# A cross-attention layer with layer norm: first transfer of context and key weights split in two, an input block queued ahead of output weights, one batch's masks cast at once, and GpSimd passes tied behind VectorE passes

## The chip, the core and the metric

The kernel runs on one core of a Trainium2 chip. The core has five engines with a queue of instructions each, done in order: TensorE (PE, matrix products; PEld is its loading of weights), VectorE (DVE), ScalarE (ACT), GpSimd (POOL) and SyncE (SP, which here only issues DMAs). ACT and POOL issue some DMAs too. An engine waits for another by semaphores. PE writes to PSUM, which has eight banks of 128 x 512 float32; everything else lives in SBUF, and inputs and outputs in HBM.

The metric is the device time of one execution in microseconds. Verdicts compare medians of several executions; the profile comes from one execution whose own time is given beside it.

## What is computed

```python
def _L0_xattn_ref(q, k, v, wq, wk, wv, wo, gamma, beta, mask):
    B, S, D, H = (2, 1024, 512, 16); HD = D // H
    Bq, Lq, _ = q.shape; Lk = k.shape[1]
    qs = (q @ wq).reshape(Bq, Lq, H, HD).transpose(0, 2, 1, 3)
    ks_ = (k @ wk).reshape(Bq, Lk, H, HD).transpose(0, 2, 1, 3)
    vs = (v @ wv).reshape(Bq, Lk, H, HD).transpose(0, 2, 1, 3)
    scores = jnp.einsum('bhqd,bhkd->bhqk', qs, ks_) / jnp.sqrt(jnp.float32(HD))
    scores = jnp.where(mask[:, None, :, :], -jnp.inf, scores)
    attn_w = jax.nn.softmax(scores, axis=-1)
    attn = jnp.einsum('bhqk,bhkd->bhqd', attn_w, vs)
    attn = attn.transpose(0, 2, 1, 3).reshape(Bq, Lq, H * HD)
    out = attn @ wo + q
    mu = jnp.mean(out, axis=-1, keepdims=True)
    var = jnp.mean((out - mu) ** 2, axis=-1, keepdims=True)
    return (out - mu) / jnp.sqrt(var + EPS) * gamma + beta
```

`q` is x, 4 x 2048 x 512 float32; `k` and `v` are both the context, 4 x 77 x 512; the mask is 4 x 2048 x 77. There are 16 heads of 32.

## The kernel before

**Tiles and stages.** The 8192 rows of x make 64 tiles of 128 rows, 16 to a batch. Two tiles are a block (32 blocks, `b`), four are a group of 512 rows (16 groups, `g`), for which q is computed at one go.

**Split products.** Products with wq, wk, wv and wo are made in three parts for accuracy: each operand is split into a high part (cast to fp32r) and a low part (what the cast lost), and high x high, high x low and low x high are summed in a bank. A split is a cast, mostly by ACT, and a subtraction by DVE or POOL.

**The order.** Nothing is scheduled by a planner at build time. The text `ORDER` lists words in the order in which instructions are issued; each engine does its own in that order. `SLOTS` lists the buffer that each allocation takes, `"mm"` those of the eight PSUM banks. A word is a letter, a number and sometimes a part: `T39.2` is part 2 (a quarter of the heads) of tile 39. The words that matter here, with the engine and the line in the profile:

- `l0 l2` (SP, L707): load the second input block, group 1, into `stage_a`, over the staged context and keys' weights; `g` (SP, L263): load half of a later group. `i` (ACT, L266): its cast. `j` (POOL, L270): its low part. A number k is group k // 2, half k % 2, so `i2 i3 j2 j3` are group 1, `i4 i5 j4 j5` group 2, `j23` half of group 11.
- `R` (SP, L359): load a quarter of wo for the low part, 256 KB; `p` (POOL's DMA, L362): load wo's high part, cast on the way, 1 MB; `G` (DVE, L368): wo's low part. `A` (SP, L347), `C` (POOL's DMA, L350), `F` (DVE, L356): the same for wv. `E` (POOL, L353): a copy that holds POOL's DMAs until wq has landed.
- `L` (SP, L377): load a batch's mask bytes. `M28.4` (DVE, L386): turn those of tiles 28 to 31 into a bf16 bias. `M` has no dependence on POOL.
- `H`, `Q` (PE, L276): a visit, a quarter of a group's q; `I`, `q` (DVE, L292 and L290): its copy out of PSUM. `H0 H2 I0 I2` are the second half of group 0.
- `S` (PE, L403): scores of a tile, into four banks. `T` (DVE, L420): add the mask, take the maxima and copy to SBUF, which frees the bank of that quarter. `e` (ACT, L435): exponentials and their sums. `r` (DVE, L445): reciprocals. `n` (POOL, L450): scale by them. `t` (DVE, L471): transpose in blocks of 32. `P`, `U`: DMAs that regroup the result, mostly SP's.
- `B` (PE, L327): values; `D` (DVE, L336): their copy. `V` (PE, L496): values' product of a block, in two banks. `a` (ACT, L525) and `b` (DVE, L529): its high and low parts. `O` (PE, L552): output product of a tile. `x` (SP): load x for the residual. `+` (DVE, L561): add it. `s` (DVE, L575 and L576): moments. `v` (POOL, L581 to L584): 1 / sqrt of a block's variances. `k` (ACT, L590): scale by them. `f` and `)` (POOL, L593 and L596): gamma and beta. `w` (SP): store.

**The start.** Ahead of `ORDER`, PE runs nine matmuls on a constant. SP queues, in this order, four chunks of `kin` (context and wk side by side, 308 + 512 columns each, into `stage_a`), the first half block of x with wq in between, the mask of batch 0, and the other half block. Chunk by chunk the context and wk are split (L666 to L672) and `keys_part` makes the keys' products; then wq and x are split and `q` of the first 256 rows is made. The tail of that part is:

```python
    for c in range(0, NC_D, 2):
        split(xh[0][:, c : c + 2, BLK:], xl[0][:, c : c + 2, BLK:], f0[c][:, 1])
    for m in range(0, NG, 2):
        nc.scalar.copy(qd[0][:, m, :BLK], pq0[m][:, :BLK])
        nc.vector.tensor_copy(qd[0][:, m + 1, :BLK], pq0[m + 1][:, :BLK])
```

Then the words of `ORDER` follow. Its first ones are:

```
R1 R0 R3 E l0 l2 C2 C0 C1 C3 g5 M4.4 A0 M0.1 M12.4 A1 M1.3 A3 M8.4 A2 H2 p i3 g4 i2 S0 I2 j2 S1 T0.1 e0.1
```

**Around 276 us** the order has `r35 O26 a14.0 b14.0 n34 t34 O27 +27 v12 P16.7s Q43 q43 M44.4 e36.2 k24 a14.1 b14.1 n35 t35 i22 s27 V15 x28 )23 f24 e36.1 S37 T37.3 T37.2 k25 a15.0 b15.0 T37.1`, five regrouping and store words, `M40.4 j23 f25 )25`, and on to `e37.1 +26 s26 v13`, `T37.0`, `j22`, `n36`, `k27 a15.1 b15.1 )24 S38`.

Of the kernel before, what the change touches and what calls it, by code (L numbers as in the profile page):

```python
# [8 lines left out]
F32 = mybir.dt.float32  # L9
# [4 lines left out]
ALU = mybir.AluOpType  # L14
# [35 lines left out]
R1 R0 R3 E l0 l2 C2 C0 C1 C3 g5 M4.4 A0 M0.1 M12.4 A1 M1.3 A3 M8.4 A2 H2 p i3 g4 i2 S0 I2 j2 S1 T0.1 e0.1  # L50
T0.2 H0 T0.0 j3 e0.0 T1.0 T0.3 e0.2 T1.1 Q4 T1.2 e0.3 F0 T1.3 I0 e1.2 r0 n0 S2 q4 e1.0 S3 T2.3 T2.0 Q7 T2.2 L1 R2 F3
Q6 F1 G1 x1 e1.1 F2 i5 j5 g7 t0 e1.3 Y1 r1 n1 T3.1 T3.2 T2.1 q7 B0 T3.3 i4 t1 P0.7s P0.3s P0.10s j4 D0 Z3.s Z0.s G2 G3
G0 g6 P0.11s Q5 q6 q5 e2.0 e2.3 e3.3 e2.2 e2.1 e3.1 i7 j7 B2 r2 T3.0 e3.0 S4 T4.2 T4.0 T4.3 n2 T4.1 e4.2 D2 P0.1s e3.2
r3 n3 e4.3 e4.0 P0.6s P0.5s i6 j6 e4.1 g8 P0.8s Z2.s P0.9s P0.4s B1 D1 P0.2s t2 P0.0s t3 P1.10s P1.11s S6 T6.0 T6.3
T6.2 P1.2s r4 P1.3s P1.1s Q10 T6.1 e6.0 Q8 q8 n4 e6.2 e6.1 e6.3 q10 Q9 q9 Z1.s S5 T5.0 e5.0 P1.6s P1.7s P1.5s P1.0s
P1.4s P1.8s t4 S7 T7.1 e7.1 T7.3 T7.2 e7.2 P1.9s r6 n6 T7.0 e7.0 T5.2 Y0 Z15.s Z10.s Q14 Q11 g9 q11 T5.1 T5.3 e7.3 r7
n7 t6 x7 Z16.s e5.2 Q13 q14 i8 e5.3 S9 T9.1 Z4.s V1 t7 x0 x3 P3.9s P3.11s P3.4s Z14.s a1.0 b1.0 x2 e5.1 r5 n5 j8 q13
a1.1 b1.1 T9.2 T9.0 Z5.s V0 a0.0 b0.0 T9.3 P3.0s P3.5s e9.1 e9.0 a0.1 e9.3 i9 j9 P3.10s P3.7s P3.8s O2 t5 M28.4 S8
T8.1 e8.1 T8.2 e8.2 e9.2 +2 b0.1 s2 O3 +3 P2.5s T8.3 e8.3 T8.0 e8.0 P3.2s r9 s3 v1 P2.3s P3.3s Z11.s k3 P2.0s P3.1s
# [15 lines left out]
P9.4s a7.0 b7.0 e20.3 P8.6s Q24 q24 P9.9s O13 e21.0 i15 j15 a7.1 v5 e21.1 e22.1 )9 +13 s13 Q26 q26 b7.1 e20.1 r20 n20
w8 e21.3 e21.2 T22.3 r21 k10 f10 O12 +12 s12 t20 n21 e22.0 w5 P9.1s P9.6s f4 )4 e22.3 P9.7s w9 Q27 q27 e22.2 P9.10s
P9.3s S23 T23.1 T23.3 T23.2 e23.3 P9.0s v6 g17 P9.5s x15 V8 a8.0 a8.1 i16 e23.1 k11 S24 t21 P10.1s O15 r22 b8.1 n22
b8.0 P10.0s w4 x17 T24.0 T24.2 e24.2 O17 O16 T24.1 e23.2 T23.0 e23.0 T24.3 +15 P10.9s x14 x16 t22 P10.4s k12 r23 e24.3
S25 T25.0 T25.3 T25.2 k13 +17 s17 e25.2 e24.1 P10.3s )10 P10.8s f11 P10.6s P10.2s P10.11s n23 t23 T25.1 V9 a9.1 a9.0
# [10 lines left out]
e31.0 r31 n31 P14.1s P14.4s e32.2 i21 P14.8s w19 k20 f20 j21 )20 k21 f21 e32.1 T32.3 e32.3 w16 x25 P14.5s P14.2s T32.0  # L90
t30 P14.0s P14.10s x24 e32.0 O23 +23 O22 +22 b12.0 s23 Q38 q38 S33 T33.2 T33.3 T33.1 V13 i20 S34 e33.2 P14.9s t31
P15.5s P14.7s P14.11s s22 v11 )21 e33.3 T34.1 T33.0 e33.0 O24 a13.0 b13.0 j20 r32 n32 +24 k22 e33.1 a13.1 T34.2 k23
T34.0 g22 P15.9s P15.6s e34.2 P15.11s P15.7s r33 T34.3 e34.3 e34.0 f22 Q39 q39 b13.1 n33 Q36 q36 t32 O25 +25 S35 T35.2
T35.3 e34.1 g23 P15.10s w20 w21 P15.1s P15.4s P15.0s f23 T35.1 T35.0 e35.1 V14 P15.8s )22 r34 P15.3s P15.2s t33 P16.2s
P16.4s S36 T36.3 s24 T36.2 s25 T36.0 e35.2 e35.0 i23 e35.3 T36.1 r35 O26 a14.0 b14.0 n34 t34 O27 +27 v12 P16.7s Q43
q43 M44.4 e36.2 k24 a14.1 b14.1 n35 t35 i22 s27 V15 x28 )23 f24 e36.1 S37 T37.3 T37.2 k25 a15.0 b15.0 T37.1 P16.6s
P16.1s P16.3s P16.8s w22 P16.0s M40.4 j23 f25 )25 x29 x26 P16.11s e36.0 e36.3 e37.1 +26 s26 v13 e37.3 e37.2 w23
P16.10s x31 T37.0 r36 O29 +29 s29 j22 O28 +28 s28 P16.9s P17.10s w25 n36 x32 P16.5s k27 a15.1 b15.1 )24 S38 T38.3
T38.1 T38.0 k26 e37.0 T38.2 e38.3 e38.2 r37 n37 f26 )26 Q41 q41 Q42 q42 e38.1 t36 P17.11s g25 P17.0s P17.2s Q40 q40
S39 T39.1 P17.4s T39.2 T39.0 T39.3 e38.0 t37 e39.1 x30 r38 f27 v14 n38 i25 g24 )27 P17.6s P17.9s V16 a16.1 e39.0 e39.2  # L100
S40 T40.1 P17.3s i24 P17.5s w24 T40.0 b16.1 T40.2 O30 O31 T40.3 P18.5s P17.1s P17.7s P17.8s a16.0 P18.10s Q44 w26
P18.1s e40.0 e39.3 b16.0 O32 k29 e40.2 P18.8s x34 +30 j24 +31 s31 e40.3 s30 v15 k31 t38 r39 P18.6s n39 q44 w27 S41
T41.0 P18.11s f29 P18.9s e40.1 V17 P18.4s L3 x33 g26 j25 f31 Q45 t39 P18.2s P19.10s e41.0 T41.2 P18.0s P18.3s a17.1
T41.3 P19.7s e41.3 k30 k28 +32 T41.1 P19.4s P18.7s q45 S42 T42.1 )31 a17.0 e42.1 e41.2 e41.1 T42.0 T42.3 r40 s32 O33
# [70 lines left out]
def xattn_layernorm(  # L175
# [92 lines left out]
    def split_xT(g, c):  # L268
        l = once(xl, g, [P, NC_D, GRP], F32R, "xtl")
        nc.gpsimd.tensor_tensor(l[:, c : c + 2], fx.pop((g, c)), xh[g][:, c : c + 2].bitcast(F32), ALU.subtract)  # L270
# [517 lines left out]
```

## Time and profile before

| | |
|---|---|
| median of 3 executions | 513.0 us (512.81, 513.0, 514.88) |
| the profiled execution | 513.14 us |
| its span, first to last instruction | 511.3 us, mean granted clock of PE 0.998 |
| busy: PE, PEld | 499.2 us (98%), 383.9 us (75%) |
| busy: DVE, ACT, POOL | 470.3 us (92%), 464.6 us (91%), 421.1 us (82%) |
| DMA | 110.85 MB, mean 217 GB/s |

The span is shorter than the time of its execution by 1.8 us, which lie before the first and behind the last instruction. In rows of the trace the first number is the start in us from the span's start, the second the length in us; then the engine (SPq is SP's queue of DMAs), the line, the operation, what it writes and reads, the shapes and the count of instructions that the row merges. Brackets give the engine's idle time before it and what ended it. In rows of waits, "PE sc L403 <- DVE q L290" is PE's instruction of line 403 waiting for DVE's of line 290. Ends of matmuls are modelled, so the distance between starts says more than a matmul's length.

### The profile page before, as it was taken

How to read it: one execution, taken by the hardware profiler on the slowest of the kernel's cores; microseconds unless marked ns; L12 is line 12 of the kernel's file. 1: busy time of each engine (PE TensorE's matmuls, PEld its weight loads, DVE VectorE, ACT ScalarE, POOL GpSimd, SP SyncE). 2: the span in 40 equal slices, each digit the busy share in tenths (PEclk: the TensorE clock that was granted, in tenths of full speed). 3: DMA queues.
4: the chain of work that ended last, by engine and by line, in shares of the span. 5: the costliest groups of instructions: out<-in, count | busy, mean ns of one | idle time of the engine just before them, and what ended most of it. 6: DMA issues, size and time to landing. Idle time of an engine off the chain costs nothing. (4 is left out here: it accounts for less than half of the span.)

```text
span 511.3 us, 20308 instructions
## 1 busy us (share of the span) xinstructions
PE 499.2 (98%) x6833; PEld 383.9 (75%) x6833; DVE 470.3 (92%) x2563; ACT 464.6 (91%) x2222; POOL 421.1 (82%) x387
## 2 busy tenths in 40 slices
PE   8998999999999999999999999999999999999994
PEld 6976777777777877777777777778777777777773
DVE  5799889988999989988989998999999999999997
ACT  6698999999999999998999999999999999989720
POOL 2556656876897999998898899898999899898896
PEclk9999999999999999999999999999999999999999
DMA  8954786878686986779877868787879677699655
GB/s 307 390 196 131 173 220 163 230 177 225 192 245 182 267 222 169 229 210 249 245 223 210 228 172 252 178 219 204 247 201 235 189 217 240 192 228 252 162 185 216
DMA packets 58781, 110.85 MB, mean 217 GB/s; under 512 B 9462, under 2 KB 11278, under 8 KB 58678
## 3 DMA queue, kind: packets, MB, share of 16 engines
q1 hardware_dynamic: 55222, 102.75, 72.0%
q0 software_dynamic: 2496, 5.77, 4.0%
q8 instruction: 54, 0.88, 0.8%
q10 hardware_dynamic: 960, 1.05, 0.8%
q14 instruction: 49, 0.40, 0.3%
HBM read 41.79 MB, written 16.78 MB: 115 GB/s over the span
## 5 line engine op out<-in xcount | busy, mean ns | idle before, releaser
L435 ACT ACTIVATE pbuf<-pbuf,nm 128x77 f32<-128x77 f32 x1024 | 352.7, 352 | 8.7 <-DVE nm L420 8.0
L435 ACT ACTIVATION_READ_ACCUMULATOR pbuf<-pbuf,nm 128x1 f32 x1024 | 197.1, 193 | 0.0
L420 DVE CUSTOM_DVE_ANT_0 pbuf<-sc,mb 128x77 f32<-128x77 f32 x1024 | 170.0, 231 | 6.4 <-PE sc L403 4.6
L450 POOL TENSOR_TENSOR pbuf<-pbuf,ri 128x1232 f32<-128x1232 f32 x63 | 142.3, 2261 | 34.8 <-DVE ri L445 29.6
L552 PE MATMUL po<-woh,AH 128*128 128x512 f32 x256 | 104.0, 406 | 0.1
L471 DVE STREAM_TRANSPOSE B<-pbuf 128x1280 f32<-128x1280 f32 x64 | 95.8, 1498 | 8.2 <-POOL pbuf L450 7.2
L276 PE MATMUL pq<-xth,wqh 128*128 128x512 f32 (+1 forms) x256 | 100.6, 393 | 0.9 <-DVE nm L420 0.6
L552 PE MATMUL po<-wol,AH 128*128 128x512 f32 x256 | 100.0, 391 | 0.0
L552 PE MATMUL po<-woh,AL 128*128 128x512 f32 x256 | 99.9, 390 | 0.0
L276 PE MATMUL pq<-xtl,wqh 128*128 128x512 f32 (+1 forms) x256 | 98.2, 383 | 0.0
L276 PE MATMUL pq<-xth,wql 128*128 128x512 f32 (+1 forms) x256 | 98.1, 383 | 0.0
L420 DVE DVE_READ_ACCUMULATOR2_ANT nm<- 128x1 f32 x1024 | 84.4, 82 | 0.0
L270 POOL TENSOR_TENSOR xtl<-xtf,xth 128x1024 fp32r<-128x1024 f32 x28 | 67.4, 2408 | 9.6 <-issue 4.8
L593 POOL TENSOR_TENSOR o<-o,gam 128x512 f32<-128x512 f32 x56 | 72.1, 1292 | 2.9 <-ACT o L590 2.7
L596 POOL TENSOR_TENSOR o<-o,bet 128x512 f32<-128x512 f32 x56 | 72.0, 1289 | 1.4
L403 PEld LDWEIGHTS sc<-kct,q 32*64 32x64 f32 x4096 | 51.8, 130 | 24.4 <-issue 11.5
L403 PE MATMUL sc<-kct,q 32*64 32x77 f32 x4096 | 61.7, 238 | 2.2 <-DVE q L290 1.6
L496 PE MATMUL pa<-PT,vsb 96*32 96x256 f32 x992 | 59.7, 382 | 0.0
L552 PEld LDWEIGHTS po<-woh,AH 128*128 128x128 f32 x256 | 48.0, 188 | 15.3 <-issue 3.8
L276 PEld LDWEIGHTS pq<-xth,wqh 128*128 128x128 f32 x256 | 48.1, 188 | 14.7 <-issue 2.1
L552 PEld LDWEIGHTS po<-woh,AL 128*128 128x128 f32 x256 | 48.1, 188 | 10.5
L276 PEld LDWEIGHTS pq<-xth,wql 128*128 128x128 f32 x256 | 48.1, 188 | 9.6
(99 smaller groups left out, 640.3 us busy)
## 6 DMA issues: line engine op xcount, KB each, us to landing
PT<-B SPq DMA_DIRECT2D x343, 128.0 KB
xtf<-xT SPq DMA_DIRECT2D x28, 512.0 KB
o<-x SPq DMA_DIRECT2D x56, 256.0 KB
out<-o SPq DMA_DIRECT2D x56, 256.0 KB
PT<-B POOLq DMA_DIRECT2D x25, 128.0 KB, 4.8
stage_a<-kin SPq DMA_DIRECT2D x4, 410.0 KB
xtf<-xT SPq DMA_DIRECT2D x4, 256.0 KB
wq_f<-wq SPq DMA_DIRECT2D x4, 256.0 KB
```

Of the source, the lines that this page charges most:

```text
L270: nc.gpsimd.tensor_tensor(l[:, c : c + 2], fx.pop((g, c)), xh[g][:, c : c + 2].bitcast(F32), ALU.subtract)
L276: nc.tensor.matmul(pq, w[:, c, m * P : (m + 1) * P], r[g][:, c, rs], start=(n == 0), stop=(n == 11))
L403: mm = nc.tensor.matmul(sc[j][r0 : r0 + SR, g * NK : (g + 1) * NK], qs[q, g, rs.start + r0 : rs.start + r0 + SR], kct[q, g, t // TPB, keys ...
L420: nc.vector.tensor_tensor_reduce(pb[:, h // 2, (h % 2) * NK : (h % 2 + 1) * NK], scs[t][j][:, g * NK : (g + 1) * NK], mb[:, t % TPB, keys_ ...
L435: nc.scalar.activation(pb[:, h // 2, (h % 2) * NK : (h % 2 + 1) * NK], pb[:, h // 2, (h % 2) * NK : (h % 2 + 1) * NK], AF.Exp, bias=nmax[t ...
L450: nc.gpsimd.tensor_tensor(pv, pv, rv.to_broadcast((P, NP, 2, NK)), ALU.mult)
L471: nc.vector.transpose(bt.rearrange("p c q r -> p q c r"), pbuf[t % NPB].rearrange("p q (c r) -> p q c r", c=5),)
L496: nc.tensor.matmul(pas[b, g // 2][HD * j : HD * (j + 1), (g % 2) * BLK : (g % 2 + 1) * BLK], vsb[:, 2 * b // TPB, h % 2, HD * (h // 2) : H ...
L552: nc.tensor.matmul(pos[t], a[:, c, rs], w[:, c, :], start=(first and c == 0 and n == 0), stop=(c == NC_D - 1 and n == 2),)
L593: nc.gpsimd.tensor_tensor(od[t], od[t], gam, ALU.mult)
L596: nc.gpsimd.tensor_tensor(od[t], od[t], bet, ALU.add)
```

## The change

- The first chunk of `kin` comes in two transfers: the context and the first half of wk's columns, then the other half. Its wk is cast and split by halves, and the keys' products of chunk 0 are made for the first two of four banks (all three parts), then for the other two.
- `E l0 l2` stand ahead of `R1 R0 R3` in the order.
- The masks of batch 0 are made by one instruction over its 16 tiles, ahead of the copies of the first q, in place of five words `M`.
- A new wait: after each word `F`, `G` or `M`, the next word `j`, `n`, `f` or `)` waits for it to end. `split_xT`, `split_wv`, `split_wo`, `mask_bias`, `normalise`, `gain` and `shift` return their instruction for that.
- `SLOTS`: from the scores of tile 1 on, banks 6 and 7 are exchanged; the last of "PT" is changed, and isn't taken by any allocation.

```diff
 ORDER = """
-R1 R0 R3 E l0 l2 C2 C0 C1 C3 g5 M4.4 A0 M0.1 M12.4 A1 M1.3 A3 M8.4 A2 H2 p i3 g4 i2 S0 I2 j2 S1 T0.1 e0.1
+E l0 l2 R1 R0 R3 C2 C0 C1 C3 g5 A0 A1 A3 A2 H2 p i3 g4 i2 S0 I2 j2 S1 T0.1 e0.1
...
     def keys_part(pks, c):
         terms = ((woh, 0), (woh, 1), (wol, 0))
-        steps = [(n, m) for n in range(3) for m in range(NG)] if c == 0 else [(n, m) for m in range(NG) for n in range(3)]
+        steps = [(n, m) for m in range(NG) for n in range(3)]
+        if c == 0:
+            steps = [(n, m + i) for m in (0, 2) for n in range(3) for i in (0, 1)]
...
+    def wait_for(later, earlier, reason):
+        info = mybir.DependencyInfo(mybir.DependencyClass.Sync, mybir.DependencyReason.DATA)
+        tc.add_manual_dep(later.ins, earlier.ins.name, info, reason=reason)
...
-    for c in range(NC_D):
+    half = NB * NK + D // 2
+    nc.sync.dma_start(kin_f[:, 0, :half], kin[:, 0, :half])
+    nc.sync.dma_start(kin_f[:, 0, half:], kin[:, 0, half:])
+    for c in range(1, NC_D):
         nc.sync.dma_start(kin_f[:, c], kin[:, c])
...
         if c == 0:
             nc.vector.tensor_copy(ctx_s[c][0], ctx_f)
-            nc.scalar.copy(woh[:, c], wk_f)
-            nc.vector.tensor_tensor(ctx_s[c][1], ctx_f, ctx_s[c][0].bitcast(F32), ALU.subtract)
-            nc.vector.tensor_tensor(wol[:, c], wk_f, woh[:, c].bitcast(F32), ALU.subtract)
+            for h in range(2):
+                cols = slice(h * D // 2, (h + 1) * D // 2)
+                nc.scalar.copy(woh[:, c, cols], wk_f[:, cols])
+                if h == 0:
+                    nc.vector.tensor_tensor(ctx_s[c][1], ctx_f, ctx_s[c][0].bitcast(F32), ALU.subtract)
+                nc.vector.tensor_tensor(wol[:, c, cols], wk_f[:, cols], woh[:, c, cols].bitcast(F32), ALU.subtract)
...
+    mask_bias(0, TPB)
     for m in range(0, NG, 2):
         nc.scalar.copy(qd[0][:, m, :BLK], pq0[m][:, :BLK])
...
+    shared = None
     for word in ORDER.split():
...
         else:
-            ops[op](int(k or 0), int(part or 0))
+            ins = ops[op](int(k or 0), int(part or 0))
+            if op in "FGM":
+                shared = ins
+            elif shared and op in "jnf)":
+                wait_for(ins, shared, "VectorE's pass over two tiles of SBUF is begun ahead of GpSimd's")
+                shared = None
```

More of the change, by code (lines that the diff above doesn't have):

```diff
@@ L55 @@
[L55 to L59, printed above, removed]
@@ L75 @@
[L75 to L79, printed above, removed]
@@ L90 @@
[L90 to L104, printed above, removed]
@@ new lines @@
+T22.1 T22.2 s10 g16 T22.0 s11 x12 P8.7s P9.11s e20.0 f8 f9 )8 P9.8s P9.2s P8.0s P9.4s a7.0 b7.0 e20.3 P8.6s Q24 q24
+P9.9s O13 e21.0 i15 j15 a7.1 v5 e21.1 e22.1 )9 +13 s13 Q26 q26 b7.1 e20.1 r20 n20 w8 e21.3 e21.2 T22.3 r21 k10 f10 O12
++12 s12 t20 n21 e22.0 w5 P9.1s P9.6s f4 )4 e22.3 P9.7s w9 Q27 q27 e22.2 P9.10s P9.3s S23 T23.1 T23.3 T23.2 e23.3 P9.0s
+v6 g17 P9.5s x15 V8 a8.0 a8.1 i16 e23.1 k11 S24 t21 P10.1s O15 r22 b8.1 n22 b8.0 P10.0s w4 x17 T24.0 T24.2 e24.2 O17
+O16 T24.1 e23.2 T23.0 e23.0 T24.3 +15 P10.9s x14 x16 t22 P10.4s k12 r23 e24.3 S25 T25.0 T25.3 T25.2 k13 +17 s17 e25.2
@@ new lines @@
+P15.1s P15.4s P15.0s f23 T35.1 T35.0 e35.1 V14 P15.8s )22 r34 P15.3s P15.2s t33 P16.2s P16.4s S36 T36.3 s24 T36.2 s25
+T36.0 e35.2 e35.0 i23 e35.3 T36.1 r35 O26 a14.0 b14.0 n34 t34 O27 +27 v12 P16.7s Q43 q43 M44.4 e36.2 k24 a14.1 b14.1
+n35 t35 i22 s27 V15 x28 )23 f24 e36.1 S37 T37.3 T37.2 k25 a15.0 b15.0 T37.1 P16.6s P16.1s P16.3s P16.8s w22 P16.0s
+M40.4 j23 f25 )25 x29 x26 P16.11s e36.0 e36.3 e37.1 +26 s26 v13 e37.3 e37.2 w23 P16.10s x31 T37.0 r36 O29 +29 s29 j22
+O28 +28 s28 P16.9s P17.10s w25 n36 x32 P16.5s k27 a15.1 b15.1 )24 S38 T38.3 T38.1 T38.0 k26 e37.0 T38.2 e38.3 e38.2
@@ new lines @@
+r37 n37 f26 )26 Q41 q41 Q42 q42 e38.1 t36 P17.11s g25 P17.0s P17.2s Q40 q40 S39 T39.1 P17.4s T39.2 T39.0 T39.3 e38.0
+t37 e39.1 x30 r38 f27 v14 n38 i25 g24 )27 P17.6s P17.9s V16 a16.1 e39.0 e39.2 S40 T40.1 P17.3s i24 P17.5s w24 T40.0
+b16.1 T40.2 O30 O31 T40.3 P18.5s P17.1s P17.7s P17.8s a16.0 P18.10s Q44 w26 P18.1s e40.0 e39.3 b16.0 O32 k29 e40.2
+P18.8s x34 +30 j24 +31 s31 e40.3 s30 v15 k31 t38 r39 P18.6s n39 q44 w27 S41 T41.0 P18.11s f29 P18.9s e40.1 V17 P18.4s
+L3 x33 g26 j25 f31 Q45 t39 P18.2s P19.10s e41.0 T41.2 P18.0s P18.3s a17.1 T41.3 P19.7s e41.3 k30 k28 +32 T41.1 P19.4s
@@ L355, in split_wv @@
     def split_wv(c):
-        nc.vector.tensor_tensor(wvl[c], stage_b[:, 0, c], wvh[c].bitcast(F32), ALU.subtract)
+        return nc.vector.tensor_tensor(wvl[c], stage_b[:, 0, c], wvh[c].bitcast(F32), ALU.subtract)
     def load_wo(c):
@@ L367, in split_wo @@
     def split_wo(c):
-        nc.vector.tensor_tensor(wol[:, c], stage_b[:, 1, c], woh[:, c].bitcast(F32), ALU.subtract)
+        return nc.vector.tensor_tensor(wol[:, c], stage_b[:, 1, c], woh[:, c].bitcast(F32), ALU.subtract)
     def idents():
@@ L391, in early_waits @@
         for part in parts[int(after[1:])] if after[0] == "V" else ():
-            info = mybir.DependencyInfo(mybir.DependencyClass.Sync, mybir.DependencyReason.DATA)
-            tc.add_manual_dep(mm.ins, part.ins.name, info, reason="values' product waits ahead of the scores")
+            wait_for(mm, part, "values' product waits ahead of the scores")
     def scores(t):
@@ L592, in gain @@
     def gain(t):
-        nc.gpsimd.tensor_tensor(od[t], od[t], gam, ALU.mult)
+        return nc.gpsimd.tensor_tensor(od[t], od[t], gam, ALU.mult)
     def shift(t):
-        nc.gpsimd.tensor_tensor(od[t], od[t], bet, ALU.add)
+        return nc.gpsimd.tensor_tensor(od[t], od[t], bet, ALU.add)
     def store(t):
```

161 lines of the change are left out of this document (86 added, 75 removed).

## The prediction

> **What bounds the kernel now.** I read the busy times by stage first, then TensorE's own waits, then the order of time on each engine at those waits. The cuts at 62, 276 and 306 us are mine; behind a stretch and its length stand the busy times of PE, PE's weight loads, DVE, ACT and POOL, the clock, the DMA share and GB/s.
>
> ```profile
> 0.00:62.00 62.00, 58.13 (x788) 47.76 (x789) 51.71 (x261) 49.77 (x223) 32.77 (x30) 1.00 0.77 243
> 276.00:306.00 30.00, 29.41 (x416) 22.57 (x415) 29.59 (x163) 29.53 (x136) 27.40 (x25) 1.00 0.77 213
> ```
>
> TensorE (PE) is the bound: it idles 3.9 us of the first 62 and 0.6 of the 30 behind 276. Only what moves a PE wait, or makes one, moves the end. VectorE (DVE) and ScalarE (ACT) are nearly full from 276 to 306, so little there absorbs a delay.
>
> ```profile
> PE sc L403 <- DVE q L290: 1.6, 2, 1.3
> PE pk L300 <- ACT woh L667: 0.5, 1, 0.5
> PE pq L276 <- DVE nm L420: 0.6, 1, 0.6
> ```
>
> The columns are the total in us, the times and the longest. PE's waits are few and short: 1.3 and 0.3 us for copies of q, 0.5 at the first keys' product, 0.6 for the maxima that free a bank; these 2.7 us are 0.5% of the time.
>
> **First chunk in two transfers.** The rows are PE's, DVE's and ACT's, in order of time.
>
> ```profile
> 5.08 0.83 PE L300 MATMUL pk<-ctx_h,woh 128*128 128x308 f32 x4 [0.45 <-ACT woh L667]
> 7.17 0.41 PE L300 MATMUL pk<-ctx_h,wol 128*128 128x308 f32 x1
> 6.42 0.69 DVE L249 TENSOR_TENSOR wol<-stage_a,woh 128x512 fp32r<-128x512 f32 x1
> 5.42 0.45 ACT L248 CAST ctx_h<-stage_a 128x308 fp32r<-128x308 f32 x1 [0.39 <-DMA stage_a<-kin]
> ```
>
> PE can start some 0.45 us sooner, right behind the warm-up. But the low part of chunk 1's weights is ready at 6.42 + 0.69 = 7.11, in a chain that starts with that chunk's landing (ACT waits for it until 5.42), and the matmul that takes it starts right then, at 7.17. The same bytes stand ahead of chunk 1, so PE waits there instead: 0 gained. Bounds: 0.45 gained if chunk 1 also comes earlier, 0.45 lost if the extra issue delays it. I take 0, the row at 7.17.
>
> **Second input block ahead of three output weights.**
>
> ```profile
> 9.86 1.67 SPq L359 DMA_DIRECT2D stage_b<-wo  x3
> 7.43 0.69 DVE L249 TENSOR_TENSOR wol<-stage_a,woh 128x512 fp32r<-128x512 f32 x1
> 18.00:21.00 3.00, 3.00 (x48) 2.87 (x54) 1.69 (x7) 0.84 (x2) 0.00 (x0) 1.00 1.16 397
> 20.16 1.99 ACT L266 CAST xth<-stage_a 128x1024 fp32r<-128x1024 f32 x2 [2.16 <-DMA stage_a<-xT]
> 22.24 4.75 POOL L270 TENSOR_TENSOR xtl<-stage_a,xth 128x1024 fp32r<-128x1024 f32 x2 [5.92 <-ACT xth L266]
> 26.16 1.39 DVE L356 TENSOR_TENSOR wvlAH<-stage_b,wvh 128x512 fp32r<-128x512 f32 x1
> 28.09 0.68 DVE L292 COPY q<-pq 128x512 f32<-128x512 f32 x1
> 28.83 1.67 PE L403 MATMUL sc<-kct,q 32*64 32x77 f32 x128 [0.37 <-DVE q L292]
> ```
>
> Three transfers of 256 KB at 397 GB/s are 2.0 us, just the time that ACT is idle. The casts `i3 i2` move from 20.16 to about 18.15, GpSimd's (POOL) two splits from 22.24 to about 20.2, and end at 24.9 instead of 26.99. `F0` at 26.16 then meets no POOL pass. It took 1.39 where its kind takes 0.68, ending 0.55 behind POOL's end, so 0.7 goes. The copy behind it ends 0.7 sooner, before PE is free: the 0.37 wait goes, and q's next product takes its place. **Gain 0.4** (0 if the block lands no sooner, 0.5 at most). On SP's queue the block passes three transfers, to 9.86. It overwrites `stage_a`, whose chunk 2 DVE has read by 7.43 + 0.69 = 8.1, so SP is not held there. The weights land where the block did, about 20, and `G1` reads them at 32.93.
>
> **Masks of batch 0 at once.**
>
> ```profile
> 17.27 0.42 DVE L694 COPY q<-pq 128x256 f32<-128x256 f32 x1 [0.88 <-PE pq L680]
> 18.33 1.23 DVE L386 TENSOR_SCALAR mb<-m 128x384 bf16<-128x384 uint8 x5
> ```
>
> The 1.23 us move in front of the copy of q, into the 0.88 us of idle time there; the copies end 0.3 later or not at all. PE has a whole visit of q (`H2`, 24 matmuls) to do before its scores use them: 0. If that cover were gone, 0.3.
>
> **The ties early on.** A word `F`, `G` or `M` (a DVE pass) is now waited for by the next POOL word of `j n f )`.
>
> ```profile
> 32.79 2.49 POOL L270 TENSOR_TENSOR xtl<-xtf,xth 128x1024 fp32r<-128x1024 f32 x1 [1.53 <-ACT xth L266]
> 32.93 2.90 DVE L368 TENSOR_TENSOR wol<-stage_b,woh 128x512 fp32r<-128x512 f32 x1
> 43.14 1.88 DVE L368 TENSOR_TENSOR wol<-stage_b,woh 128x512 fp32r<-128x512 f32 x3
> 44.94 1.28 DVE L290 COPY q<-pq 128x512 f32<-128x512 f32 x2
> 44.54 0.39 PE L403 MATMUL sc<-kct,q 32*64 32x77 f32 x16
> 46.27 0.82 PE L403 MATMUL sc<-kct,q 32*64 32x77 f32 x48 [1.34 <-DVE q L290]
> ```
>
> `G1` began 0.14 us behind POOL's `j5` and took 2.90, 2.2 more than its kind. Now `j5` waits for `F2`, which DVE does behind `F1` and `G1`. With the 0.7 from above DVE is 2.9 sooner: it ends `G1` at 35.83 - 2.9 = 32.9 and `F2` at 33.6. `j5` runs from 33.6 to 36.1, 0.8 later than before; `n1`, queued behind it, takes 2.26 (as at 276.47 below) to 38.4; `j4`, another split of 2.4, runs to 40.8. DVE's `t1` waits for `n1`. Its place is a transpose (1.49) and a copy (0.68) ahead of `G2`, that is 43.14 - 2.9 - 2.1 = 38.1, so it waits 0.3. `G2` then comes at 40.5 and meets the last 0.3 of `j4`. Of 2.9 us 2.3 are left: the two copies of q end at 46.22 - 2.3 = 43.9. PE reaches them at 44.1 and no longer waits: a quarter of the scores' 64 matmuls was through ahead of the wait, the other 48 would have started some 0.25 after 44.54, not at 46.27. **Gain 1.5** (bounds 0 and 1.6).
>
> **The ties later.** POOL, DVE, ACT, PE around 276 us; last, all passes over masks.
>
> ```profile
> 276.47 2.26 POOL L450 TENSOR_TENSOR pbuf<-pbuf,ri 128x1232 f32<-128x1232 f32 x1
> 281.31 2.40 POOL L270 TENSOR_TENSOR xtl<-xtf,xth 128x1024 fp32r<-128x1024 f32 x1
> 285.03 1.29 POOL L596 TENSOR_TENSOR o<-o,bet 128x512 f32<-128x512 f32 x1
> 288.17 0.20 POOL L581 TENSOR_TENSOR rn<-mv,small 128x2 f32<-128x2 f32 x1 [1.84 <-DVE mv L576]
> 279.53 0.67 DVE L386 TENSOR_SCALAR mb<-m 128x384 bf16<-128x384 uint8 x1
> 280.72 1.49 DVE L471 STREAM_TRANSPOSE B<-pbuf 128x1280 f32<-128x1280 f32 x1
> 285.39 1.15 DVE L386 TENSOR_SCALAR mb<-m 128x384 bf16<-128x384 uint8 x1
> 289.72 0.82 ACT L590 ACTIVATE o<-o,rn 128x512 f32<-128x512 f32 x1 [0.40 <-POOL rn L584]
> 290.44 0.57 ACT L525 CAST AH<-pa 128x512 fp32r<-128x512 f32 x1
> 291.79 0.66 DVE L529 TENSOR_TENSOR AL<-pa,AH 128x512 fp32r<-128x512 f32 x1
> 299.45 0.08 DVE L420 DVE_READ_ACCUMULATOR2_ANT nm<- 128x1 f32 x1
> 299.88 0.83 PE L403 MATMUL sc<-kct,q 32*64 32x77 f32 x54
> ...
> L386 DVE TENSOR_SCALAR mb<-m x17: 204/354/2109, 18.3 to 446.5; 128x384 bf16<-128x384 uint8 x15, 128x96 bf16<-128x96 uint8 x1, 128x288 bf16<-128x288 uint8 x1
> ```
>
> Here POOL is ahead of the written order. `n35` began at 276.47, but the word before it that ties it, `M44.4`, comes to DVE at 279.53, behind a copy of q that waits for PE. `n35` now starts at 279.53 + 0.35 = 279.9, 3.4 late. Queued behind it on POOL stand `)23 f24 j23 f25 )25 v13`; on DVE `t35` waits for it until 282.2, 1.5 late. That puts the next mask, `M40.4`, at 286.9 to 287.25 (0.7 late in the end, since no POOL pass stretches it now), and PE's 0.6 us wait for a bank grows by 0.7. `j23` is tied to `M40.4`: 287.3 instead of 281.31. With its 2.40, two passes of 1.29 behind it and 1.55 for `v13` (288.17 to ACT's 289.72) that is 293.9. ACT's `k27` waited for just that already, so it is 4.2 late, and with it `a15.1`. `a15.1` ended at 291.0, DVE's `b15.1` began 0.8 later, at 291.79, so it is 3.4 late; DVE has next to no idle time from there to the maxima of tile 39, whose second group ends at 299.53 and frees a bank of `S40`, 0.35 before PE starts it at 299.88. PE comes 3.4 - 0.35 = **3.1 late** in all, and PE has nothing to catch up with. Bounds: 0.7 if ACT and DVE swallow `k27`'s delay, 4.2 if none of it is absorbed.
>
> The other ten masks: the longest, 2.11 us, is one that POOL's `n45`, begun just ahead, blocked; the tie gives DVE 2.11 - 0.35 = 1.75 and delays POOL by less, both where PE has no wait. The rest are past before POOL's next word, or shift POOL by up to 2 us in stretches where it idles afterwards: 0 each, 0.3 either way together. `SLOTS` only renames two banks.
>
> By the Trainium skill (SBUF — State Buffer, § Who interferes with whom) a VectorE instruction with two SBUF inputs and a GpSimd one that reads SBUF exclude each other, and whichever comes second waits for the first one's end. The trace agrees (2.90 against 0.68 us). The rule speaks against a tie: the exclusion alone costs the second at most the first one's length, while the tie also charges POOL for the way of DVE to the pass, 3.4 us at `n35`; without that charge the time would be the first rival's.
>
> **Sum.** The profiled execution took 513.14 us (span 511.3 and 1.8 around it), 0.14 above the median of 513.0. 513.14 + 0 - 0.4 + 0 - 1.5 + 3.1 = 514.3; beside the median, **514.2**.
>
> **Rivals.**
> - *The late ties are hidden.* If POOL's delay at 276 is swallowed, only the early gain is left: 513.0 - 1.9 = 511.1, and 510.4 with the small waits too (0.3 at 60 us, 0.2 later). For it: POOL is idle 1.84 us before `v13` and DVE had 0.7 us of collisions to lose. Against it: ACT already waits for `v13`, and DVE is busy 29.59 of 30 us there.
> - *The output weights come late (slower).* `G1` reads two transfers of them: SP's, now behind the input block, and POOL's, whose rows are these (issue; size and time to landing):
>
> ```profile
> 15.51 0.81 POOL L362 DMA_DIRECT2D woh<-wo  x1
> woh<-wo POOLq DMA_DIRECT2D x1, 1024.0 KB, 15.3
> ```
>
>   It landed at 15.5 + 15.3 = 30.8; `G1` is now to start at 32.2. If the new order of transfers delays it by over 1.4 us, `G1` waits, and by its tie `F2` also `j5`, `n1`, `t1` and the copies of q. 0.2 us more use up PE's margin, and from there each us costs one: at 33.9 the 1.5 is lost, 513.0 - 0.4 + 3.1 = 515.7. For it: 30.8 is near. Against it: the block and the weights swap places well ahead of that, so the bytes in front of this transfer stay the same.
> - *The early parts do nothing*, since the block lands no sooner: the 0.4 and a part of the 1.5 stay away, 514.8 to 515.3. DMA at 397 GB/s with that block at the end of its queue speaks against it.
>
> **Chances.** A measurement of this kernel tells about 0.5% (2.6 us) from no change, so the edges are 510.4 and 515.6. Forecast, 513.2 to 515.3: 0.52, all within. Late ties hidden: 0.27, of which 0.10 below 510.4. Output weights late: 0.13, of which 0.10 above. Early parts idle: 0.08, of which 0.04 above. So faster 0.10, same 0.76, slower 0.14. The range reaches to both first rivals: 510.7 to 516.0; the likeliest case alone is 513.2 to 515.3.
>
> **What would show it.** Right: PE's first keys' matmul near 4.6 but chunk 1's third no sooner; ACT's cast of the second block near 18.2; the passes of L368 and L356 all at 0.68; no PE wait near 46; then POOL idle some 3 us before `n35`, ACT waiting some 3 us for `rn` before a L590, and a PE wait of over 2 us at the scores of tile 40. Wrong: `n35` starting right behind `v12`, or ACT's wait there staying at 0.4.

## The result and the profile after

| | before | after |
|---|---|---|
| median, us | 513.16 (6 runs, 512.81 to 514.88) | 522.28 (6 runs, 519.84 to 523.0) |
| profiled execution, us | 513.14 | 522.27 |
| its span, us | 511.3 | 520.2 |
| its mean granted clock of TensorE | 0.998 | 0.989 |

The ratio is 1.0167, with a 95% interval of 1.0143 to 1.0191. The changed kernel is slower by 9.1 us, where 1.2 were forecast and 516.0 was the upper end of the range. Three single executions of 693 to 1689 us (one of the run with `M52.4` alone, two of the kernel before) are slow ones and stand outside the comparisons below.

The stretches with the cuts of the prediction, in the kernel after:

```profile
0.00:62.00 62.00, 60.57 (x794) 50.40 (x795) 50.59 (x265) 51.59 (x232) 32.57 (x30) 1.00 0.80 249
276.00:306.00 30.00, 26.97 (x401) 20.03 (x400) 25.28 (x141) 25.33 (x119) 23.98 (x22) 1.00 0.65 185
```

In the first 62 us PE is busy 60.57 us instead of 58.13: the early part gains. In the 30 us behind 276 PE idles 3.0 us instead of 0.6, and DVE, ACT and POOL are all less busy than before: each waits for another.

Then the two largest groups of waits that are new in kind, and PE's waits over 1 us behind its warm-up (total, times, longest):

```profile
POOL pbuf L455 <- DVE mb L388: 9.2, 5, 3.5
POOL o L601 <- DVE mb L388: 6.3, 2, 4.5
...
PE sc L408 <- DVE nm L425: 1.8, 3, 1.1
PE po L557 <- ACT pbuf L440: 1.6, 1, 1.6
PE sc L408 <- DVE o L566: 1.2, 1, 1.2
PE po L557 <- DVE nm L425: 1.2, 2, 0.9
PE sc L408 <- DVE q L290: 1.1, 1, 1.1
```

POOL now waits for masks (`mb`), which no POOL word did before: L455 is the normalisation `n`, L601 the word `)`. The longest, 4.5 us, is at a mask to which the prediction gave a cost of 0.

Where the time went is read by following the same matmul through both traces. First of before, then of after, PE's rows:

```profile
17.79 0.28 PE L276 MATMUL pq<-xth,wqh 128*128 128x256 f32 x1
47.02 0.50 PE L327 MATMUL pv<-wvh,ctx_h 128*128 128x512 f32 x1
300.76 0.50 PE L552 MATMUL po<-woh,AH 128*128 128x512 f32 x1
370.24 0.63 PE L496 MATMUL pa<-PT,vsb 96*32 96x256 f32 x7
458.82 0.50 PE L552 MATMUL po<-woh,AH 128*128 128x512 f32 x1
461.74 0.48 PE L403 MATMUL sc<-kct,q 32*64 32x77 f32 x26
```

```profile
18.70 0.28 PE L276 MATMUL pq<-xth,wqh 128*128 128x256 f32 x1
29.28 1.76 PE L408 MATMUL sc<-kct,q 32*64 32x77 f32 x128
45.80 0.51 PE L329 MATMUL pv<-wvh,ctx_h 128*128 128x512 f32 x1
302.73 0.50 PE L557 MATMUL po<-woh,AH 128*128 128x512 f32 x1
373.48 0.42 PE L501 MATMUL pa<-PT,vsb 96*32 96x256 f32 x4
465.74 0.77 PE L557 MATMUL po<-woh,AH 128*128 128x512 f32 x1 [1.57 <-ACT pbuf L440]
471.12 0.39 PE L408 MATMUL sc<-kct,q 32*64 32x77 f32 x16
```

After minus before: +0.9 at the first products of q, +0.45 at the scores that stood at 28.83, -1.2 at the values' products, +2.0 behind 300 us, +3.2 at 370, +6.9 at 459 and +9.4 at 462. So the start loses 0.9, the early part gains 2.1, and from there 3.2 us are lost around 276 to 303, 1.3 more by 370 and 6.1 more by 462. The last step, 2.5 us within twelve matmuls, is no wait at all: see the section on the clock.

### The profile page after: what moved, and what is told of

Same layout as the page of the kernel before. It is cut to its first block, busy times and chain, and to the rows that moved or that the text cites. A ratio compares the mean times of both kernels' runs of the same rounds, so it can differ in the third digit from the quotient of the medians.

```text
span 520.2 us, 20318 instructions
## 1 busy us (share of the span) xinstructions
PE 504.3 (97%) x6833; PEld 387.7 (75%) x6833; DVE 463.7 (89%) x2560; ACT 464.5 (89%) x2223; POOL 420.2 (81%) x387
## 3 DMA queue, kind: packets, MB, share of 16 engines
q10 hardware_dynamic: 960, 1.05, 0.8%
## 5 line engine op out<-in xcount | busy, mean ns | idle before, releaser
L440 ACT ACTIVATION_READ_ACCUMULATOR pbuf<-pbuf,nm 128x1 f32 x1024 | 200.2, 196 | 0.0
L455 POOL TENSOR_TENSOR pbuf<-pbuf,ri 128x1232 f32<-128x1232 f32 x63 | 142.0, 2257 | 38.3 <-DVE ri L450 23.4
L601 POOL TENSOR_TENSOR o<-o,bet 128x512 f32<-128x512 f32 x56 | 71.9, 1289 | 7.7 <-DVE mb L388 6.3
L408 PE MATMUL sc<-kct,q 32*64 32x77 f32 x4096 | 62.9, 238 | 4.3 <-DVE nm L425 1.8
L595 ACT ACTIVATE o<-o,rn 128x512 f32<-128x512 f32 x56 | 44.7, 815 | 13.8 <-POOL rn L589 12.4
```

Source lines behind the costliest of these rows:

```text
L408: mm = nc.tensor.matmul(sc[j][r0 : r0 + SR, g * NK : (g + 1) * NK], qs[q, g, rs.start + r0 : rs.start + r0 + SR], kct[q, g, t // TPB, keys ...
L440: nc.scalar.activation(pb[:, h // 2, (h % 2) * NK : (h % 2 + 1) * NK], pb[:, h // 2, (h % 2) * NK : (h % 2 + 1) * NK], AF.Exp, bias=nmax[t ...
L455: return nc.gpsimd.tensor_tensor(pv, pv, rv.to_broadcast((P, NP, 2, NK)), ALU.mult)
L595: nc.scalar.activation(o, o, AF.Identity, bias=rn[:, 1, tt : tt + 1], scale=rn[:, 0, tt : tt + 1])
L601: return nc.gpsimd.tensor_tensor(od[t], od[t], bet, ALU.add)
```

## The experiments

Theory, from these traces: the ties on four masks (`M44.4` and `M40.4`, `M52.4`, `M60.4`) hold POOL up to the place that DVE has reached, and each is paid by PE; the ties on `F` and `G` gain what was predicted; the split of the first chunk costs 0.9. The main rival: the new start and the new order of transfers shift the engines against each other, and the ties cost little in themselves. In each session of the runs below the kernel before, on the same chip, had a median of 513.1 to 513.4. A time is set against the run with the ties of `F` and `G` alone, 511.85, where nothing else is said; ratios are to the kernel before.

### No tie, and the ties of F and G alone

```diff
-            if op in "FGM":
+            if op in "":
```

> The changed kernel without any of its ties; the first chunk, the order and the masks at once stay. Theory (the ties on masks cost some 9 us in all, those on F and G gain 1.5, the split of the first chunk costs 0.9 behind chunk 1's later landing, the input block gains 0.45): 522.3 - 9.0 - 0.3 + 1.7, so 513 to 514.5, near the kernel before, with PE's wait at the q copies near 46 back and none over 1 us later. Rival (the new start or the order of transfers disturbs the later work by itself, the ties little): 517 or more.

```diff
-            if op in "FGM":
+            if op in "FG":
```

> The changed kernel with the ties of F and G alone, those of all twelve M taken away. Theory: the early gain of 1.5 to 1.7 stays and no POOL word waits for a mask: 511.3 to 512.5, 1 to 2 below the run without ties. Rival (the ties of F and G cost as much as they bring, or the losses after 276 us come from the shifted start and not from masks): as the run without ties, or 515 and more.

Without ties: 514.11 us (10 runs, ratio 1.0016, interval 1.0003 to 1.0030). With those of `F` and `G`: 511.85 (10 runs, 0.9978, 0.9968 to 0.9987). So the rest of the change (start, order, masks at once) costs 1.0, the ties of `F` and `G` gain 2.3, and the ties of the masks cost 522.28 - 511.85 = 10.4, more than the whole loss. The main rival falls: without ties the shifted start alone ends at 514.11, not at 517 or more. The kernel with the ties of `F` and `G` alone is faster than the kernel before.

### Four masks, one place at a time

```diff
-            if op in "FGM":
+            if op in "FG" or word in ("M44.4", "M40.4"):
```

> Ties of F and G and of two masks, M44.4 and M40.4, around 276 us. Theory (each tied place costs by itself what PE lost there, 3.2 us): 3 above the run with F and G alone, 514.5 to 515.5, with PE waits over 2 us in all near 300. Rival (the loss there needs the other ties' shifts ahead of it, or is regained by 350 us): within 1 of the run with F and G alone.

```diff
-            if op in "FGM":
+            if op in "FG" or word == "M60.4":
```

> Ties of F and G and of one mask, M60.4, near 450 us. Theory (by itself it delays a word ')' of POOL by some 4 us, from there ACT, DVE and PE, and a drop of PE's clock behind it): 5 to 6 above the run with F and G alone, 516.5 to 518, with PE matmuls of O near 465 at half rate. Rival A (the clock drop has another cause than these waits, so it is not in this run): 3 to 3.5 above. Rival B (M60.4 costs only because the earlier losses have shifted the engines against each other): within 1.

`M44.4` with `M40.4`: 516.32 (4 runs, 1.0063, 1.0045 to 1.0081), 4.5 above the ties of `F` and `G`; expected were 3, and 516.32 lies above the range of 514.5 to 515.5. `M60.4`: 516.42 (4 runs, 1.0071, 1.0051 to 1.0091), 4.6 above; the lower end of what was expected is missed by little, and both of its rivals are out. The two places together explain 9.1 of the 10.4.

The profiles part these sums into waits and clock. PE's output product at 298.99 us of the run with `F` and `G` starts at 302.10 with `M44.4` and `M40.4`, 3.1 later, after 0.2 early ahead of 276; a product of q behind it, at 304.58, starts at 309.26, 4.7 later. The 1.6 us between are matmuls at half rate (see the section on the clock). With `M60.4` the product at 457.26 starts at 461.08 and the scores at 460.18 start at 465.48; PE had been 0.3 late before that place, so 3.5 us are waits and 1.5 are half rate, behind waits of 1.08 and 1.59 us. The half rate is thus there with this one mask alone, and the rival that gave it another cause falls on this too.

How one tie costs that much is seen at `M60.4`. With the ties of `F` and `G` alone, rows of POOL, DVE and POOL:

```profile
440.91 1.29 POOL L601 TENSOR_TENSOR o<-o,bet 128x512 f32<-128x512 f32 x1
444.93 0.35 DVE L388 TENSOR_SCALAR mb<-m 128x384 bf16<-128x384 uint8 x1
445.93 2.27 POOL L455 TENSOR_TENSOR pbuf<-pbuf,ri 128x1232 f32<-128x1232 f32 x1
```

POOL runs `)46` four us before DVE comes to the mask, although the order is written the other way round, and the mask takes its plain 0.35 us: there was no collision to save. In the kernel after, rows of DVE, POOL, ACT and again DVE:

```profile
450.56 0.36 DVE L388 TENSOR_SCALAR mb<-m 128x384 bf16<-128x384 uint8 x1
451.07 1.29 POOL L601 TENSOR_TENSOR o<-o,bet 128x512 f32<-128x512 f32 x1 [4.55 <-DVE mb L388]
453.89 1.52 ACT L595 ACTIVATE o<-o,rn 128x512 f32<-128x512 f32 x2 [3.54 <-POOL rn L589]
456.02 2.27 POOL L455 TENSOR_TENSOR pbuf<-pbuf,ri 128x1232 f32<-128x1232 f32 x1
458.32 1.51 DVE L476 STREAM_TRANSPOSE B<-pbuf 128x1280 f32<-128x1280 f32 x1 [3.98 <-POOL pbuf L455]
```

POOL stands still for 4.55 us, with `v24` (the factor `rn`), three transfers and `n58` queued behind `)46`. ACT waits 3.54 us for `rn`, and DVE, the very engine that POOL was made to wait for, waits 3.98 us for `n58`. From there the maxima, and so the banks of PE's next scores, are late.

Now the two masks at 276 us apart:

```diff
-            if op in "FGM":
+            if op in "FG" or word == "M40.4":
```

> Ties of F and G and of M40.4 alone. Without ties POOL begins j23 at 279.49 and DVE M40.4 at 283.59, so j23 would be 4.5 late, v13 behind it 3 or more. Theory (each of the two ties holds POOL by itself up to DVE's place, and j23's is the later one): 513 to 515, over half of the loss of 4.5. Rival (the loss starts with n35, as the prediction put it, through the transposes that wait for it): within 0.7 of F and G alone, 511.2 to 512.5.

```diff
-            if op in "FGM":
+            if op in "FG" or word == "M44.4":
```

> Ties of F and G and of M44.4 alone. Without ties POOL begins n35 at 274.67 and DVE ends M44.4 near 278.1, so n35 is 3.4 late and POOL's later idle 1.84 us take up half of it. Theory of M40.4: within 1 of F and G alone, 511.8 to 512.9. Rival (n35): 514 to 516.

`M40.4` alone: 515.66 (10 runs, 1.0047, 1.0032 to 1.0061), 3.8 above the ties of `F` and `G`, and 0.7 above what was expected at most. `M44.4` alone: 513.17 (10 runs, 0.9996, 0.9986 to 1.0005), 1.3 above; that is 0.3 more than the theory of `M40.4` allowed and 0.8 less than its rival asked for. So `j23` behind `M40.4` carries most of that loss. In the two profiles, neither of which shows half rate here, the shares are nearer: against the run with `F` and `G`, PE loses 1.7 us from 276 to 299 us with `M40.4`, and 0.8 with `M44.4`. With `M40.4` alone POOL's and ACT's rows are:

```profile
277.98 1.40 POOL L598 TENSOR_TENSOR o<-o,gam 128x512 f32<-128x512 f32 x1
283.93 2.39 POOL L270 TENSOR_TENSOR xtl<-xtf,xth 128x1024 fp32r<-128x1024 f32 x1 [4.54 <-issue]
290.46 0.82 ACT L595 ACTIVATE o<-o,rn 128x512 f32<-128x512 f32 x1 [3.09 <-POOL rn L589]
```

POOL waits 4.54 us in front of `j23` (the view names no releaser; the only edit here is that tie, and DVE's mask ends at 283.8), and ACT's `k27` waits 3.09 us for `rn`. With `M44.4` alone POOL waits 3.49 us in front of `n35`, but ACT's wait for `rn` at that place is only 0.45: POOL had idle time later on (1.85 us in front of `v13` with the ties of `F` and `G` alone), and none is left there.

The third place, and the other eight masks:

```diff
-            if op in "FGM":
+            if op in "FG" or word == "M52.4":
```

> Ties of F and G and of one mask, M52.4, near 373 us. Theory (each of the four masks that POOL comes ahead of costs by itself; the run with all ties is 10.4 above the one with F and G alone, of which M44.4 with M40.4 took 4.5 and M60.4 4.6): 1 to 2 above F and G alone, 512.9 to 513.9, with POOL's n47 waiting some 3 us for the mask. Rival (DVE's late transpose there came from transfers shifted by the ties ahead, not from this mask): within 0.5 of F and G alone.

```diff
-            if op in "FGM":
+            if op in "FG" or word in ("M44.4", "M40.4", "M52.4"):
```

> Ties of F and G and of M44.4, M40.4 and M52.4. M52.4 alone cost nothing, yet all ties together cost 10.4 where M44.4 with M40.4 (4.5) and M60.4 (4.6) leave 1.3 open. Theory (the delay made at 276 us still shifts DVE against POOL and the queues when M52.4 comes, so that POOL waits 3 us for it there): 1 to 2 above the run with M44.4 and M40.4, 517.3 to 518.3. Rival (the rest is clock drops or scatter, not M52.4): as that run, 516.3.

```diff
-            if op in "FGM":
+            if op in "FGM" and word not in ("M44.4", "M40.4", "M52.4", "M60.4"):
```

> Ties of F and G and of the eight masks other than M44.4, M40.4, M52.4 and M60.4. Theory (these eight are past before POOL's next word, or delay it where nothing waits): within 0.5 of the run with F and G alone, 511.4 to 512.4. Rival (some of them cost, above all M48.4, where POOL's n45 waited 0.8 us): 513 or more.

`M52.4` alone: 511.56 (9 runs), the same as without it, so the theory failed for this mask; POOL waits 0.65 us for it here. With `M44.4` and `M40.4` ahead of it: 517.26 (5 runs, 515.0 to 518.15), 0.9 above those two; the runs scatter too much to call that shown, and in the profiled one POOL waits 0.36 us for that mask, not 3.27 as in the kernel after. What makes the wait long there, where 1.3 us more are lost by 370 us, stays open. The other eight: 511.8 (8 runs), free, as expected, although POOL waits 1.24 to 1.86 us for a mask in front of three words near 125 to 134 us of this run. `M48.4`, whose collision was the longest in the trace before, is among the eight. PE does gain 0.5 us behind it in the profile (two products of q start 9.2 us apart, at 350.57 and 359.73, which are 9.7 apart with `F` and `G` alone); the median doesn't show it. What is left of the 10.4 beside 4.5, 4.6 and 0.9 is 0.4, within the scatter.

### The first chunk

```diff
-    half = NB * NK + D // 2
-    nc.sync.dma_start(kin_f[:, 0, :half], kin[:, 0, :half])
-    nc.sync.dma_start(kin_f[:, 0, half:], kin[:, 0, half:])
-    for c in range(1, NC_D):
+    for c in range(NC_D):
         nc.sync.dma_start(kin_f[:, c], kin[:, c])
...
-            if op in "FGM":
+            if op in "FG":
```

The casts, splits and products of chunk 0 went back to their form of before with it.

> Ties of F and G alone, and the first chunk of context and keys' weights in one transfer as before; the order of the input block and the masks at once stay. Theory (the second transfer makes chunk 1 land 0.9 later, which PE pays): 0.7 to 1.0 below the run with F and G alone, 510.8 to 511.2, with ACT's cast of chunk 1 back near 5.4 us. Rival (chunk 1 is late for another reason): as the run with F and G alone, 511.9.

```diff
-    nc.sync.dma_start(kin_f[:, 0, half:], kin[:, 0, half:])
+    nc.scalar.dma_start(kin_f[:, 0, half:], kin[:, 0, half:])
...
-            if op in "FGM":
+            if op in "FG":
```

> Ties of F and G alone, and the second transfer of the first chunk issued by ScalarE's queue in place of SP's. Theory (SP's extra issue of 0.46 us delays chunk 1, the rest of the 0.9 is transfers of smaller rows): half of the loss comes back, 511.3 to 511.6, chunk 1's cast near 5.9. Rival (the bytes in front of chunk 1 alone set its landing): no change, 511.9, its cast near 6.3.

One transfer: 511.0 (5 runs, 0.9964, 0.9951 to 0.9978). Two transfers, the second from ScalarE's queue: 510.96 (6 runs, 0.9961, 0.9946 to 0.9977), where half of the loss was expected back. By the medians either takes back the 0.9. ACT's cast of chunk 1 in the kernel after, with one transfer, and with the second queue, three rows of three traces:

```profile
6.32 0.45 ACT L248 CAST ctx_h<-stage_a 128x308 fp32r<-128x308 f32 x1 [1.99 <-DMA stage_a<-kin]
```

```profile
5.04 0.45 ACT L248 CAST ctx_h<-stage_a 128x308 fp32r<-128x308 f32 x1 [0.45 <-DMA stage_a<-kin]
```

```profile
5.16 0.45 ACT L248 CAST ctx_h<-stage_a 128x308 fp32r<-128x308 f32 x1 [0.36 <-DMA stage_a<-kin]
```

With both transfers in, and the same bytes in pieces of the same size, chunk 1 lands 1.2 us sooner when SP does not issue the second piece. The cast starts at 5.75 to 6.78 us in all ten profiles with that issue on SP's queue, and at 5.04 to 5.42 in the four without it. So neither the bytes nor the size of the rows delays chunk 1, but the second piece's place on SP's queue. Why an issue of 0.46 us there becomes some 1 us at the landing was not tried.

The profiles show less of the gain than the medians: the first product of q of the group's second half starts at 18.55 with `F` and `G` alone, at 18.28 with one transfer and at 18.10 with the other queue, against 17.79 before. With one transfer chunk 2 came late instead (its cast at 7.58, 6.43 before). Landings in the first 10 us scatter by about 1 us between profiles, so here the medians count, not one trace.

### Ties that cost nothing

The last experiment keeps the rule of the ties and moves the words instead, so that DVE is at the mask when POOL comes to the word behind it. Three things follow from the rule: `M44.4` and `M40.4` stand side by side, so one wait, of `n35` for `M40.4`, replaces their two; `j23` waits for no mask any more; and `n34` is put ahead of them so that it isn't tied. The second piece of the first chunk is issued from ScalarE's queue.

```diff
-r34 P15.3s P15.2s
+r34 n34 P15.3s P15.2s
...
-T36.2 s25 T36.0
+T36.2 s25 M44.4 M40.4 T36.0
...
-a14.0 b14.0 n34 t34
+a14.0 b14.0 t34
...
-Q43 q43 M44.4 e36.2
+Q43 q43 e36.2
...
-w22 P16.0s M40.4 j23
+w22 P16.0s j23
...
-T59.2 n57 V26
+T59.2 n57 M60.4 V26
...
-T59.3 a26.1 M60.4 b26.0 )46
+T59.3 a26.1 b26.0 )46
...
-    nc.sync.dma_start(kin_f[:, 0, half:], kin[:, 0, half:])
+    nc.scalar.dma_start(kin_f[:, 0, half:], kin[:, 0, half:])
```

> All ties as in the changed kernel, with M44.4 and M40.4 put ahead of tile 36's third group of maxima and M60.4 right behind n57 in the order, n34 put behind r34, and the second transfer of the first chunk on ScalarE's queue. Theory (a tie costs what DVE lags behind POOL at that place, not by being a tie): no loss over 1 is left, 510.5 to 512, as without ties of M (510.96). Rival A (moving DVE's passes forward delays the maxima, which PE pays): 512.5 to 514. Rival B (the ties cost in themselves): over 515.

510.71 us (4 runs, 0.9953, 0.9938 to 0.9968), with a tie behind every mask but `M44.4`. Both rivals fall: a tie costs nothing by itself, and the passes moved forward cost nothing that the median shows. It is the lowest median of the study, but not distinguishable from 510.96 without ties on the masks: these ties cost nothing now, and bring nothing. The moved order without ties was not run.

The distance by which DVE lags behind POOL is not yet the price. In this run POOL still waits six times for a mask, 0.39 to 1.87 us, without a loss that the median shows, while 3.49 us at `M44.4` cost 1.3 and 4.55 us at `M60.4` cost 4.6, half rate included. What is paid is the part that POOL, and the engines that wait for it, do not make up before PE needs the result.

### The clock

In the kernel after, twelve matmuls of the output run from 465.74 to 471.12. Rows of PE, in order of time:

```profile
461.36 0.81 PE L408 MATMUL sc<-kct,q 32*64 32x77 f32 x6
463.26 0.90 PE L408 MATMUL sc<-kct,q 32*64 32x77 f32 x58 [1.09 <-DVE nm L425]
465.74 0.77 PE L557 MATMUL po<-woh,AH 128*128 128x512 f32 x1 [1.57 <-ACT pbuf L440]
...
466.73 0.63 PE L557 MATMUL po<-woh,AL 128*128 128x512 f32 x1
467.15 0.63 PE L557 MATMUL po<-woh,AH 128*128 128x512 f32 x1
...
473.89 0.39 PE L557 MATMUL po<-wol,AH 128*128 128x512 f32 x1
474.12 0.40 PE L557 MATMUL po<-woh,AL 128*128 128x512 f32 x1
```

Start to start is 0.42 us at 466 and 0.23 at 474: half rate behind two waits of 1.09 and 1.57. The granted clock of the stretch says the same:

```profile
460.00:475.00 15.00, 12.22 (x158) 8.74 (x157) 12.92 (x98) 12.21 (x67) 13.37 (x15) 0.77 0.68 183
```

Behind three waits at 300 us the rate stays full in the kernel after; in the profile with `M44.4` and `M40.4` alone, with nearly the same waits, it drops there. First the kernel after, then that one:

```profile
300.55 0.35 PE L408 MATMUL sc<-kct,q 32*64 32x77 f32 x4 [1.14 <-DVE q L290]
301.28 0.31 PE L408 MATMUL sc<-kct,q 32*64 32x77 f32 x2 [0.38 <-DVE nm L425]
301.91 0.89 PE L408 MATMUL sc<-kct,q 32*64 32x77 f32 x58 [0.32 <-DVE nm L425]
...
304.00 0.39 PE L557 MATMUL po<-woh,AL 128*128 128x512 f32 x1
```

```profile
299.92 0.35 PE L408 MATMUL sc<-kct,q 32*64 32x77 f32 x4 [1.09 <-DVE q L290]
...
303.42 0.63 PE L557 MATMUL po<-wol,AH 128*128 128x512 f32 x1
303.85 0.63 PE L557 MATMUL po<-woh,AL 128*128 128x512 f32 x1
```

In the profiles with `M40.4` alone and with the three masks it stays full too, behind waits of 1.05 and 1.11, 0.37 and 0.38, and 0.32 us. So the same waits are followed by half rate in one profile and not in three others. That this also varies between the runs of one kernel is likely, but not shown. For it: with `M40.4` alone the three runs with a mean clock of 0.990 took 516.2 to 517.2 us, the three with more than 0.993 took 513.2 to 514.9, and a clock lower by 0.005 over 515 us is 2.6 us of clock, the size of the gap. Against it: with `M60.4` alone a run with 0.989 took 516.21 and one with 0.995 took 517.65. And the mean takes in the last microseconds, where the clock falls in the kernel before too (0.91 from 500 to 511 us) and PE has little left to do; there it was 0.79 in the profile with `M40.4`, which ran at 0.995 in the mean.

The Trainium skill (TensorE: Matmul & The Clock Gate, § Part 1: The HAM clock gate) has the clock at half or full, falling after an idle window of some 3.4 us that runs freely. Half or full agrees (0.42 and 0.23 us from start to start), and so does the different sequel of the same waits; but a whole idle window wasn't needed here, since 58 short matmuls of the scores stand between the two waits and neither wait is longer than 1.6 us.

## Why the prediction was wrong, step by step

- **First chunk: 0 forecast, 0.9 lost; wrong.** The step is "The same bytes stand ahead of chunk 1, so PE waits there instead: 0 gained", with 0.45 lost as its worse bound. Bytes were not what counted: the extra issue on SP was, and between these two traces it delayed the landing by twice its own length (6.32 instead of 5.42). PE's third matmul of chunk 1 started at 8.07 instead of 7.17. By medians the term is 0.9 as well, from 511.85 to 511.0 and 510.96.
- **Input block ahead of the output weights: 0.4 forecast, 0.45 found in the trace** (from +0.9 to +0.45). ACT's casts came at 18.80 instead of the forecast 18.15, with the start 0.9 late; `F0` took 0.69. It wasn't tried alone.
- **Masks at once: 0, as forecast.** One pass of 0.95 at 16.42, with no PE wait behind it. It wasn't tried alone.
- **Early ties: 1.5 forecast, 1.7 in the trace, 2.3 between the medians without and with them; mechanism right, size a little low.** The 2.3 lie above the upper bound of 1.6; a wait of 0.26 us at 60.6, which the sum left out, is gone too. The row that carried it is DVE's `G1`, 0.69 us instead of 2.90:

```profile
33.38 0.69 DVE L370 TENSOR_TENSOR wol<-stage_b,woh 128x512 fp32r<-128x512 f32 x1
...
43.48 1.28 DVE L290 COPY q<-pq 128x512 f32<-128x512 f32 x2
```

  The copies of q end at 44.76, and PE's wait there is gone.
- **Late ties around 276: 3.1 forecast, 3.2 in the trace, 4.5 as a median; mechanism and place right.** The chain is the one named: `n35` and `j23` held, `v13` late, ACT waiting for `rn` in front of `k27`, then the scores of tile 40. Only its last link differs: PE waits 1.14 us there for a copy of q, and 0.70 for the maxima, which alone were named. POOL's and ACT's rows of the kernel after:

```profile
278.69 2.25 POOL L455 TENSOR_TENSOR pbuf<-pbuf,ri 128x1232 f32<-128x1232 f32 x1 [3.50 <-DVE mb L388]
...
292.67 0.81 ACT L595 ACTIVATE o<-o,rn 128x512 f32<-128x512 f32 x1 [3.08 <-POOL rn L589]
```

  The term holds for a run whose clock doesn't fall behind the waits: with these two masks alone the waits cost 3.3 in the profile, and half rate 1.6 on top, which the sum didn't have.
- **The other masks: "0 each, 0.3 either way together"; this step failed, and it is the main one.** It said that they "are past before POOL's next word, or shift POOL by up to 2 us in stretches where it idles afterwards". True of eight, and of `M52.4` by itself; `M60.4` shifts POOL by 4.55 us, and costs 4.6. The prediction worked the lag of DVE behind POOL out at 276 us from rows, and not at 446, where the trace of before shows the two rows of `)46` and `M60.4` in the wrong order for a tie, four us apart:

```profile
442.49 1.30 POOL L596 TENSOR_TENSOR o<-o,bet 128x512 f32<-128x512 f32 x1
446.50 0.35 DVE L386 TENSOR_SCALAR mb<-m 128x384 bf16<-128x384 uint8 x1
```

- **The rate of PE behind a wait: no term at all.** A wait was priced at its length. Waits of 1 to 1.6 us close together were followed by half rate in this profile, and 2.5 us of the 9.1 went there; with `M60.4` alone it was 1.5, with `M44.4` and `M40.4` 1.6.

The sum with these terms, from medians: 513.1 + 1.0 (start, order and masks at once) - 2.3 + 4.5 + 4.6 is 520.9; the 1.4 up to 522.3 are `M52.4` in company of the others and scatter, and are not told apart. One slip of the prediction bears on nothing: by its own small waits the first rival's lower time is 511.1 - 0.5 = 510.6, not 510.4.

## What to carry to other kernels

A dependency that is added to fix the order of two engines is sure to be free only where the engine that must go first is already ahead. Compare the two start times, in a profile without the dependency, at every place that the rule touches: lags under 2 us were made up here, lags of 3.3 to 4.6 us were paid, in part or in full, and a rule that gained 2 us at three places lost 10 at a few others. If the waiting engine feeds the one waited for, both stand still, so move the earlier word forward instead of holding the later one. And an extra transfer was charged here to whatever stood behind it on its queue; another engine's queue issued it for nothing.

## What the runs showed of the hardware

PE fell to half rate (start to start 0.42 us instead of 0.23 for a 128x512 matmul) behind waits of 1.09 and 1.57 us with 58 short matmuls between them, for 3 to 5 us. Behind three waits of some 1.1, 0.4 and 0.3 us it did so in one profile and not in three others. With one more issue of 0.46 us on SP's queue the next chunk was cast at 5.75 to 6.78 us in ten profiles, against 5.04 and 5.42 with one transfer fewer, and 5.16 and 5.21 with that issue on another queue.
